# Where the residual adds of a recurrence run: two batches on GpSimd in the rounds, two on VectorE from kept states after them

## The chip, the cores and the metric

The kernel runs on one core of one Trainium2 chip. The metric is the time of one execution on the device in microseconds (us); lower is better. Before the change the median of three runs is 2685.39 us, with 2684.89 the lowest and 2687.76 the highest. The profile is that of one execution; its span, from the first to the last instruction, is 2683.1 us. Times "at 2657" are microseconds from the start of that span.

## What is computed

The input x is 4 batches of 128 channels by 64 x 64 positions, float32. Two layers follow. Layer 0 is a group norm and full self-attention over the 4096 positions, added to x. Layer 1 takes the positions as tokens: a layer norm and causal attention, added, and then a recurrence over the tokens, added as well. Cut to what the change touches:

```python
def step(yt, wx_t):
    yt = jax.nn.sigmoid(wx_t + yt @ Vt)
    return (yt, yt)
y0 = jnp.zeros((B, H), dtype=Wx.dtype)
_, ys = jax.lax.scan(step, y0, jnp.swapaxes(Wx, 0, 1))
...
t = t + _L1_attn_ref(_ln_t(t), L1_attn_Wq, L1_attn_Wk, L1_attn_Wv)
t = t + _L1_ffn_ref(_ln_t(t), L1_ffn_W, L1_ffn_V, L1_ffn_gamma, L1_ffn_beta)
```

`Wx` is the normed token times a matrix, batch-normed over all tokens. `ys` is the state after each token. What concerns us is the last sum: the state of every token is added to the token (the residual), and the sum is stored.

## The kernel before

The attention fills most of the time. It runs batch by batch in units of 256 keys for tiles of 512 queries; the scores and the weighted values go through TensorE, the exponentials through ScalarE (L441), the running sums through VectorE (L475). The reciprocals of all softmax sums are kept in `sums` (L363). The output of the attention is stored to a scratch tensor `D` in device memory (L379), and its normed product with the recurrence's input matrix takes its place in `X` (L390). Near the end of the attention `D` is loaded again into four tiles `T`, one for each batch (`residual`, L193): these are the residuals.

The recurrence stands in `chunks`. It does not walk the 4096 tokens one after the other: they are cut into `M` = 256 chunks of `L` = 16 tokens, and all 256 chunks walk together, each after a lead-in of `LEAD` = 12 tokens. A round `s`, of which there are 28 (s from -12 to 15), does one token of every chunk, for each of the four batches `b`:

- TensorE multiplies the last state by `FV` into the PSUM tile `pg` (L543),
- VectorE adds the input, `X` times `gain`, to it (L545, a fused multiply and add),
- ScalarE takes the sigmoid into the new state `Y` (L546),
- in rounds 0 to 15 the state is added to the residual in `T[b]` (L550).

The four batches are independent, so one engine works on one batch while the others work on another. Token s of chunk m lies in column 16 m + s of `T[b]`; an add of one round thus walks `T[b]` with a step of 16 elements. The states live in a pool of five buffers (`yp`), so a buffer comes free when the adds that read it are done. `lead` keeps the states of round -1.

The adds of L550 go to VectorE where `s % 4 == 3` and in the last two rounds, to GpSimd elsewhere: 20 on VectorE, 44 on GpSimd. After the last round the four tiles `T` are stored by SyncE (L553), 2 MB each. Then comes a test of the shortcut: the largest difference between the lead-in's state and the true state of the chunk before (L556 to L558), and the largest and smallest of `sums` (L564, L565). The three results are summed by TensorE (`pb`, L568) into an integer `flag` (L571). Every engine loads the flag (L580) and jumps over a slower version of the whole kernel if it is zero (L581). At the very end SyncE waits for the stores to land and a barrier closes the program.

Each engine takes its instructions in the order in which they stand in its own list. A scheduler sets that order from priorities and dependences: it had put the two maxima of `sums` (L564) far ahead of their place in the text, between the last instructions of the attention.

Of the kernel before, what the change touches and what calls it, by code (L numbers as in the profile page):

```python
# [26 lines left out]
F32 = mybir.dt.float32  # L27
AF = mybir.ActivationFunctionType
ALU = mybir.AluOpType
AX = mybir.AxisListType  # L30
PSUM = bass.MemoryType.PSUM

P = 128
# [4 lines left out]
L = 16  # L38
M = 4096 // L
LEAD = 12  # L40
# [24 lines left out]
def fast(  # L65
# [129 lines left out]
    with ExitStack() as actx:  # L195
# [317 lines left out]
        nc.vector.tensor_tensor(bias, Fbeta, bias, ALU.subtract)  # L513

    chunks(tc, X, T, gain, bias, FV, ones, sums, out, flag)


def chunks(tc, X, T, gain, bias, FV, ones, sums, out, flag):


    nc = tc.nc
    B = X.shape[1]
    with ExitStack() as ctx:
        yp = ctx.enter_context(tc.tile_pool(name="ys", bufs=5))
        keep = ctx.enter_context(tc.tile_pool(name="keep", bufs=1))
        ps_g = ctx.enter_context(tc.tile_pool(name="ps_g", bufs=1, space=PSUM))
        WX = X.rearrange("p b (c s m) -> p b c s m", s=L, c=X.shape[2] // QT)

        lead = keep.tile([P, B, M + 1], F32, name="lead")
        nc.vector.memset(lead[:, :, 0:1], 0.0)  # L530
        last = None
        for s in range(-LEAD, L):
            Y = lead[:, :, 1:] if s == -1 else yp.tile([P, B, M], F32, tag="Y", name=f"Y_{s + LEAD}")
            for b in range(B):
                wx = WX[:, b, :, s % L, :]
                y = Y[:, b, :]
                if last is None:
                    nc.scalar.activation(
                        y.rearrange("p (c m) -> p c m", c=wx.shape[1]), wx, AF.Sigmoid, bias=bias, scale=gain
                    )  # L540
                    continue
                ps = ps_g.tile([P, M], F32, tag=f"g{b}", name=f"pg_{s + LEAD}_{b}")
                nc.tensor.matmul(ps, lhsT=FV, rhs=last[:, b, :], start=True, stop=True)  # L543
                pv = ps.rearrange("p (c m) -> p c m", c=wx.shape[1])
                nc.vector.scalar_tensor_tensor(pv, wx, gain, pv, ALU.mult, ALU.add)  # L545
                nc.scalar.activation(y, ps, AF.Sigmoid, bias=bias)  # L546
                if s >= 0:
                    t = T[b].rearrange("p (m s) -> p s m", s=L)[:, s, :]
                    eng = nc.vector if s >= L - 2 or s % 4 == 3 else nc.gpsimd
                    eng.tensor_tensor(t, t, y, ALU.add)  # L550
            last = lead[:, :, :M] if s == -1 else Y
        for b in range(B):
            nc.sync.dma_start(out=out[b], in_=T[b])  # L553
        good = keep.tile([P, 4], F32, name="good")
        d = yp.tile([P, B, M - 1], F32, tag="Y", name="d")
        nc.vector.tensor_tensor(d, lead[:, :, 1:M], last[:, :, : M - 1], ALU.subtract)  # L556
        nc.vector.tensor_reduce(good[:, 0:1], d, AX.XY, ALU.max, apply_absolute_value=True)
        nc.vector.tensor_scalar(good[:, 0:1], good[:, 0:1], TOL, None, ALU.is_le)  # L558
        n = sums.shape[0]
        sums = sums.rearrange("p t j -> p (t j)")  # L560
        for i, (red, op, limit) in enumerate(
            ((ALU.max, ALU.is_le, RMAX), (ALU.min, ALU.is_ge, RMIN)), start=1
        ):
            nc.vector.tensor_reduce(good[:n, i : i + 1], sums, AX.X, red)  # L564
            nc.vector.tensor_scalar(good[:n, i : i + 1], good[:n, i : i + 1], limit, None, op)  # L565
        pb = ps_g.tile([1, 1], F32, tag="g0", name="pb")
        for i, rows in enumerate((P, n, n)):
            nc.tensor.matmul(  # L568
                pb, lhsT=good[:rows, i : i + 1], rhs=ones[:rows, 0:1], start=i == 0, stop=i == 2
            )  # L570
        nc.vector.tensor_scalar(flag, pb, -1.0, float(P + 2 * n), ALU.mult, ALU.add)  # L571
# [14 lines left out]
def whole(  # L586
# [353 lines left out]
    with ExitStack() as fctx:  # L940
# [7 lines left out]

        WX = wxp.tile([P, N, B], F32, name="WX")
        stats = wxp.tile([P, B * NQ, 6], F32, name="fstats")  # L950

        def wx_steps(b, c):
# [3 lines left out]
            nc.tensor.matmul(pw, lhsT=FW, rhs=got[0], start=True, stop=True)  # L956
            nc.scalar.copy(WX[:, ts(c, QT), b], pw)
            nc.vector.bn_stats(stats[:, b * NQ + c, :], pw)
# [21 lines left out]
        def seed(i):  # L980

            w = tmp.tile([P, TS, B], F32, tag="tmp", name=f"wn_{i}")
            nc.vector.tensor_scalar(w, WX[:, ts(i, TS), :], mv[:, 0:1], gain, ALU.subtract, ALU.mult)
            ps = ps_y.tile([P, TS, B], F32, tag="y", name=f"py_{i}")
# [8 lines left out]
        for i in range(NCH):  # L993
            Y = yp.tile([P, TS, B], F32, tag="Y", name=f"Y_{i}")
            following = None
            for s in range(TS):
                nc.tensor.matmul(
                    ps[:, s, :], lhsT=FV, rhs=last, start=False, stop=s == TS - 1, skip_group_check=True
                )
                nc.scalar.activation(Y[:, s, :], ps[:, s, :], AF.Sigmoid, bias=Fbeta)  # L1000
                last = Y[:, s, :]
                if s == TS // 2 and i + 1 < NCH:
# [44 lines left out]
```

## Time and profile before

| | before |
|---|---|
| median of 3 runs | 2685.39 us |
| span of the profile | 2683.1 us |
| TensorE busy | 2598.7 us (97%) |
| VectorE busy | 1497.6 us (56%) |
| ScalarE busy | 1118.0 us (42%) |
| GpSimd busy | 110.9 us (4%) |
| first multiply-add of round 0 (L545) | 2613.89 |
| first store issued (L553) | 2657.45 |
| flag written (L571) | 2662.89 |
| residual adds on VectorE (L550) | 20, 17.0 us |
| residual adds on GpSimd (L550) | 44, 39.3 us |

In the profile PE is TensorE, PEld its weight loads, DVE VectorE, ACT ScalarE, POOL GpSimd and SP SyncE; a `q` after the name means the engine's own queue of control instructions and DMA issues. `L550` is line 550 of the kernel. A row such as `DVE TENSOR_TENSOR T<-T,Y 128x256 f32<-128x256 f32 x3` is a group of three instructions on VectorE which write `T` and read `T` and `Y`, 128 partitions by 256 elements each; its start and the time it covers stand ahead of it. In a table by stretches each engine has its busy time and, in brackets, its number of instructions; after them come the clock that TensorE was granted, the busy share of the DMA engines, and GB/s. The chain of waits goes back from the last instruction, at each step to what released it.

### The profile page before, as it was taken

Reading aid. Unit: us, or ns where it says so; the run is one execution under the profiler, and the core shown is the slowest. Engines: PE = TensorE matmul, PEld = TensorE weight load, DVE = VectorE, ACT = ScalarE, POOL = GpSimd, SP = SyncE. Lnnn points to the kernel's source line nnn. Section 1 sums busy time; section 2 is a strip of 40 time slices with the busy share of each in tenths; the row PEclk is TensorE's granted clock in tenths of the full one; section 3 lists DMA queues with packets and bytes.
Section 4 is the critical chain, followed back from the end, with each engine's and each line's share of the span. In section 5 each row is a group of like instructions: output and inputs, shape, how many; then the busy total and the mean of one; then the engine's idle time right before and its main releaser. Section 6 shows DMA issues by size and latency. Waiting matters only on the chain.

```text
span 2683.1 us, 25668 instructions
## 1 busy us (share of the span) xinstructions
PE 2598.7 (97%) x9970; PEld 1226.6 (46%) x9970; DVE 1497.6 (56%) x2552; ACT 1118.0 (42%) x1302; POOL 110.9 (4%) x130
## 2 busy tenths in 40 slices
PE   6999999999999999999999999999999999999974
PEld 3444444445444444454444444544544444454443
DVE  4565656544555556553556565654455656555466
ACT  3444443333444444333444444334344444333353
POOL 0000000000000000000000000000000000000005
PEclk9999999999999999999999999999999999999987
DMA  3000000000000000000000000000000000100013
GB/s 133 1 1 1 1 0 12 8 5 4 5 1 1 1 1 5 12 4 9 4 1 1 1 1 1 12 8 4 5 4 1 1 0 1 67 12 8 4 67 127
DMA packets 9234, 35.81 MB, mean 13 GB/s; under 512 B 2192, under 2 KB 2960, under 8 KB 7056
## 3 DMA queue, kind: packets, MB, share of 16 engines
q1 hardware_dynamic: 6912, 33.56, 3.2%
q8 instruction: 80, 1.31, 0.2%
q10 hardware_dynamic: 2192, 0.53, 0.1%
q14 instruction: 50, 0.41, 0.0%
HBM read 17.30 MB, written 16.78 MB: 13 GB/s over the span
## 4 chain that ended last, share of the span: by engine, by line
PE 89%; DVE 7%; ACT 1%; issue 1%; DMA 0%; POOL 0%; ACTq 0%; DVEq 0%; POOLq 0%
PE av L457 47%; PE ps L428 31%; DVE tot L475 2%; DVE pg L545 1%; PE pq L319 1%; ACT s L441 1%; PE pv L313 1%; PE pk L308 1%; PE po L377 1%; PE pq L340 1%; PE pw L389 1%; DVE zt L354 1%; DVE tot L351 1%; DVE part L356 1%; PE pt L161 1%
## 5 line engine op out<-in xcount | busy, mean ns | idle before, releaser
L457 PE MATMUL av<-s,V 64*128 64x512 f32 (+3 forms) x4864 | 1361.9, 588 | 0.0
L441 ACT ACTIVATE s<-ps,shift 128x1024 f32<-128x1024 f32 (+4 forms) x796 | 808.4, 1023 | 1316.2 <-PE ps L428 1174.2
L475 DVE TENSOR_TENSOR tot<-tot,s 128x1024 f32<-128x1024 f32 (+4 forms) x796 | 878.7, 1109 | 855.5 <-ACT s L441 733.0
L428 PE MATMUL ps<-q,K 64*128 64x512 f32 (+4 forms) x3200 | 1029.3, 579 | 0.0
L457 PEld LDWEIGHTS av<-s,V 64*128 64x128 f32 (+1 forms) x4864 | 547.2, 188 | 592.3 <-issue 584.9
L428 PEld LDWEIGHTS ps<-q,K 64*128 64x128 f32 (+1 forms) x3200 | 417.0, 189 | 481.8 <-issue 470.7
L457 PE MATMUL av<-tot,V 64*128 64x512 f32 (+2 forms) x384 | 123.0, 603 | 6.1 <-DVE acc L469 5.8
L441 ACT ACTIVATE tot<-ps,shift 128x1024 f32<-128x1024 f32 (+2 forms) x68 | 71.4, 1057 | 104.3 <-PE ps L428 84.1
L155 POOL TENSOR_TENSOR rstd<-rstd,mhalf 128x4 f32<-128x4 f32 x32 | 32.2, 1007 | 1441.5 <-DVE rstd L154 1441.5
L457 PEld LDWEIGHTS av<-tot,V 64*128 64x128 f32 (+1 forms) x384 | 49.0, 188 | 70.0 <-issue 38.5
L155 POOL TENSOR_TENSOR rstd_f<-rstd_f,mhalf 128x4 f32<-128x4 f32 x32 | 33.4, 1045 | 915.3 <-DVE rstd_f L154 915.3
L543 PE MATMUL pg<-Y,FV 128*128 128x256 f32 x208 | 53.3, 418 | 16.6 <-ACT Y L546 10.0
L435 DVE TENSOR_TENSOR ps<-ps,mask 128x128 f32<-128x128 f32 x128 | 38.0, 297 | 33.8 <-PE ps L428 31.5
L174 DVE TENSOR_SCALAR V<-xt,mv,rstd 128x128 f32<-128x128 f32 x128 | 36.0, 342 | 34.4 <-POOL rstd L155 34.4
L174 DVE TENSOR_SCALAR rows<-xt_f,mv_f,rstd_f 128x128 f32<-128x128 f32 x128 | 36.7, 342 | 31.2 <-POOL rstd_f L155 31.2
L546 ACT ACTIVATE Y<-pg,bias 128x256 f32<-128x256 f32 x104 | 45.8, 474 | 18.5 <-DVE pg L545 17.9
L543 PEld LDWEIGHTS pg<-Y,FV 128*128 128x128 f32 x208 | 36.7, 205 | 34.3 <-ACT Y L546 16.9
L545 DVE SCALAR_TENSOR_TENSOR pg<-X,gain,pg 128x256 f32<-128x256 f32 x108 | 48.2, 491 | 6.9 <-PE pg L543 6.6
L354 DVE STREAM_TRANSPOSE zt<-tot 128x512 f32<-128x512 f32 x64 | 45.5, 710 | 2.1
L378 DVE TENSOR_TENSOR X<-X,po 128x512 f32<-128x512 f32 x32 | 22.0, 688 | 42.7 <-PE po L377 42.7
L351 DVE TENSOR_TENSOR tot<-tot 128x512 f32<-128x512 f32 x64 | 44.3, 692 | 2.2
L365 DVE STREAM_TRANSPOSE rt<-sums 128x512 f32<-128x512 f32 x64 | 45.0, 703 | 0.6
(127 smaller groups left out, 1133.6 us busy)
## 6 DMA issues: line engine op xcount, KB each, us to landing
X<-in_x SPq DMA_DIRECT2D x8, 1024.0 KB, 7.3
D<-X SPq DMA_DIRECT2D x32, 256.0 KB, 2.0
T<-D SPq DMA_DIRECT2D x4, 2048.0 KB, 7.8
out<-T SPq DMA_DIRECT2D x4, 2048.0 KB, 13.5
W0k<-in_w0k ACTq DMA_DIRECT2D x2, 32.0 KB, 5.1
W0q<-in_w0q ACTq DMA_DIRECT2D x2, 32.0 KB, 4.8
W0v<-in_w0v ACTq DMA_DIRECT2D x1, 64.0 KB, 5.3
W1q<-in_w1q ACTq DMA_DIRECT2D x1, 64.0 KB, 7.3
```

The source lines that it names most:

```text
L155: nc.gpsimd.tensor_tensor(dst, dst, mhalf[:, :n], ALU.pow)
L174: nc.vector.tensor_scalar(rows[:, j, :], xt[:, j, :], mv[:, j, 0:1], rstd[:, j : j + 1], ALU.subtract, ALU.mult)
L351: nc.vector.tensor_tensor(both, both, total[:, 1, :], ALU.add)
L354: nc.vector.transpose(zt.rearrange("p j a -> p (j a)"), both)
L365: nc.vector.transpose(rt.rearrange("p (j a) -> p j a", a=R), r.unsqueeze(2).to_broadcast([P, QT // R, R]))
L428: nc.tensor.matmul(ps[:, h, first[h] :], lhsT=K[layer, b][rows, ts(2 * u + h, P)], rhs=Q[t][rows, first[h] :], start=True, stop=True,)
L441: nc.scalar.activation(s[:, *a], ps[:, *a], AF.Exp, bias=shift[layer, b])
L457: nc.tensor.matmul(acc[:, first[h] :], lhsT=V[layer, b][rows, 2 * u + h, :], rhs=s[rows, h, first[h] :], start=u == 0 and h == 0, stop=u = ...
L475: nc.vector.tensor_tensor(total[:, *a], total[:, *a], s[:, *a], ALU.add)
L543: nc.tensor.matmul(ps, lhsT=FV, rhs=last[:, b, :], start=True, stop=True)
L545: nc.vector.scalar_tensor_tensor(pv, wx, gain, pv, ALU.mult, ALU.add)
L546: nc.scalar.activation(y, ps, AF.Sigmoid, bias=bias)
```

## The change

The adds are divided by batch and no longer by round. Batches 0 and 1 are added by GpSimd in every round. The states of batches 2 and 3 are written by ScalarE into a tile of their own, `later`, that keeps all 16 rounds; after the last round VectorE adds them in eight instructions of 128 x 1024 (16 rounds by 64 chunks), while the first two batches are stored. The stores of batches 2 and 3 are cut in halves, each issued when two of the eight adds are done. The differences of the test are taken batch by batch, since the last states now lie in two tiles. The words `tc.keep_in_program_order` hold an instruction at its place in the text on its engine, so that the test, with the two maxima of `sums`, comes after the eight adds. The purpose is to keep the adds out of VectorE's rounds and to start the stores of two batches without waiting for the other two.

```diff
+        half = B // 2
+        later = keep.tile([P, B - half, L, M], F32, name="later")
...
         for s in range(-LEAD, L):
-            Y = lead[:, :, 1:] if s == -1 else yp.tile([P, B, M], F32, tag="Y", name=f"Y_{s + LEAD}")
+            if s == -1:
+                Y = [lead[:, b, 1:] for b in range(B)]
+            else:
+                y = yp.tile([P, half if s >= 0 else B, M], F32, tag="Y", name=f"Y_{s + LEAD}")
+                Y = [
+                    later[:, b - half, s, :] if s >= 0 and b >= half else y[:, b, :] for b in range(B)
+                ]
...
-                nc.scalar.activation(y, ps, AF.Sigmoid, bias=bias)
-                if s >= 0:
+                nc.scalar.activation(Y[b], ps, AF.Sigmoid, bias=bias)
+                if s >= 0 and b < half:
                     t = T[b].rearrange("p (m s) -> p s m", s=L)[:, s, :]
-                    eng = nc.vector if s >= L - 2 or s % 4 == 3 else nc.gpsimd
-                    eng.tensor_tensor(t, t, y, ALU.add)
-            last = lead[:, :, :M] if s == -1 else Y
+                    nc.gpsimd.tensor_tensor(t, t, Y[b], ALU.add)
+            last = [lead[:, b, :M] for b in range(B)] if s == -1 else Y
+        for b in range(half):
+            nc.sync.dma_start(out=out[b], in_=T[b])
+        for b in range(half, B):
+            t = T[b].rearrange("p (m s) -> p s m", s=L)
+            for i in range(4):
+                cols = ts(i, M // 4)
+                tc.keep_in_program_order(
+                    nc.vector.tensor_tensor(
+                        t[:, :, cols], t[:, :, cols], later[:, b - half, :, cols], ALU.add
+                    )
+                )
+                if i % 2:
+                    cols = ts(i // 2, M * L // 2)
+                    nc.sync.dma_start(out=out[b][:, cols], in_=T[b][:, cols])
+        good = keep.tile([P, 4], F32, name="good")
+        d = keep.tile([P, B, M - 1], F32, name="d")
         for b in range(B):
-            nc.sync.dma_start(out=out[b], in_=T[b])
-        good = keep.tile([P, 4], F32, name="good")
-        d = yp.tile([P, B, M - 1], F32, tag="Y", name="d")
-        nc.vector.tensor_tensor(d, lead[:, :, 1:M], last[:, :, : M - 1], ALU.subtract)
+            tc.keep_in_program_order(
+                nc.vector.tensor_tensor(d[:, b, :], lead[:, b, 1:M], last[b][:, : M - 1], ALU.subtract)
+            )
...
-            nc.vector.tensor_reduce(good[:n, i : i + 1], sums, AX.X, red)
+            tc.keep_in_program_order(nc.vector.tensor_reduce(good[:n, i : i + 1], sums, AX.X, red))
```

More of the change, by code (lines that the diff above doesn't have):

```diff
@@ L532, in chunks @@
         for s in range(-LEAD, L):
-            Y = lead[:, :, 1:] if s == -1 else yp.tile([P, B, M], F32, tag="Y", name=f"Y_{s + LEAD}")
+            if s == -1:
[5 more added lines that the diff above has]
+                ]
             for b in range(B):
                 wx = WX[:, b, :, s % L, :]
-                y = Y[:, b, :]
                 if last is None:
                     nc.scalar.activation(
-                        y.rearrange("p (c m) -> p c m", c=wx.shape[1]), wx, AF.Sigmoid, bias=bias, scale=gain
+                        Y[b].rearrange("p (c m) -> p c m", c=wx.shape[1]), wx, AF.Sigmoid, bias=bias, scale=gain
                     )
@@ L542, in chunks @@
                 ps = ps_g.tile([P, M], F32, tag=f"g{b}", name=f"pg_{s + LEAD}_{b}")
-                nc.tensor.matmul(ps, lhsT=FV, rhs=last[:, b, :], start=True, stop=True)
+                nc.tensor.matmul(ps, lhsT=FV, rhs=last[b], start=True, stop=True)
                 pv = ps.rearrange("p (c m) -> p c m", c=wx.shape[1])
                 nc.vector.scalar_tensor_tensor(pv, wx, gain, pv, ALU.mult, ALU.add)
-                nc.scalar.activation(y, ps, AF.Sigmoid, bias=bias)
-                if s >= 0:
+                nc.scalar.activation(Y[b], ps, AF.Sigmoid, bias=bias)
+                if s >= 0 and b < half:
                     t = T[b].rearrange("p (m s) -> p s m", s=L)[:, s, :]
-                    eng = nc.vector if s >= L - 2 or s % 4 == 3 else nc.gpsimd
-                    eng.tensor_tensor(t, t, y, ALU.add)
-            last = lead[:, :, :M] if s == -1 else Y
+                    nc.gpsimd.tensor_tensor(t, t, Y[b], ALU.add)
[16 more added lines that the diff above has]
+        d = keep.tile([P, B, M - 1], F32, name="d")
         for b in range(B):
-            nc.sync.dma_start(out=out[b], in_=T[b])
-        good = keep.tile([P, 4], F32, name="good")
-        d = yp.tile([P, B, M - 1], F32, tag="Y", name="d")
-        nc.vector.tensor_tensor(d, lead[:, :, 1:M], last[:, :, : M - 1], ALU.subtract)
+            tc.keep_in_program_order(
+                nc.vector.tensor_tensor(d[:, b, :], lead[:, b, 1:M], last[b][:, : M - 1], ALU.subtract)
+            )
         nc.vector.tensor_reduce(good[:, 0:1], d, AX.XY, ALU.max, apply_absolute_value=True)
```

## The prediction

> **What bounds the kernel now.** I read the 40 slices first, then the tail by stretches, then the order of time on VectorE and GpSimd, the chain of waits, and last the queue of the store engine and the branch at the end. The slices show TensorE at 9 tenths until slice 38: the attention fills all but the last 4%, and the diff does not touch it. So only the last 115 us matter. This is the recurrence by stretches (columns: length, busy time and instructions of each engine, granted clock, DMA share, GB/s):
>
> ```profile
> 2600.00:2612.00 12.00, 12.00 (x55) 8.01 (x54) 12.00 (x28) 11.95 (x28) 0.00 (x0) 1.00 0.00 0
> 2612.00:2620.00 8.00, 8.00 (x37) 5.42 (x37) 7.98 (x19) 7.91 (x19) 5.03 (x7) 1.00 0.00 0
> 2620.00:2657.00 37.00, 26.64 (x99) 18.35 (x98) 34.52 (x66) 21.46 (x50) 34.24 (x38) 0.90 0.00 1
> ...
> 2660.00:2664.00 4.00, 0.29 (x6) 0.21 (x6) 2.50 (x4) 0.00 (x0) 0.00 (x0) 0.50 1.08 455
> 2664.00:2668.00 4.00, 0.00 (x0) 0.00 (x0) 0.00 (x0) 0.00 (x0) 0.00 (x0) 0.50 0.95 397
> ```
>
> The reader is to see three stages. Up to 2620 VectorE runs one fused multiply-add after the other and everything else fits beside it; then the residual adds join it and the rate of rounds falls; after 2657 nothing runs but four stores. VectorE in that order of time (start, length):
>
> ```profile
> 2611.60 9.01 DVE L545 SCALAR_TENSOR_TENSOR pg<-X,gain,pg 128x256 f32<-128x256 f32 x20
> 2620.52 2.84 DVE L550 TENSOR_TENSOR T<-T,Y 128x256 f32<-128x256 f32 x3
> 2623.20 1.26 DVE L545 SCALAR_TENSOR_TENSOR pg<-X,gain,pg 128x256 f32<-128x256 f32 x3
> ...
> 2657.67 0.96 DVE L545 SCALAR_TENSOR_TENSOR pg<-X,gain,pg 128x256 f32<-128x256 f32 x2
> 2658.78 1.08 DVE L550 TENSOR_TENSOR T<-T,Y 128x256 f32<-128x256 f32 x2
> 2659.77 1.21 DVE L556 TENSOR_TENSOR d<-lead,Y 128x1020 f32<-128x1020 f32 x1
> ```
>
> Three adds hold VectorE for 2.84 us while GpSimd also adds; two take 1.08 us at 2658.78, when GpSimd is done. GpSimd itself does seven in 5.73 us before the first of them:
>
> ```profile
> 2614.97 5.73 POOL L550 TENSOR_TENSOR T<-T,Y 128x256 f32<-128x256 f32 x7 [25.87 <-ACT Y L546]
> ```
>
> At the end the store queue waits (engine, waited for: total, times, longest) and every engine jumps over the fallback. The waits of SyncE:
>
> ```profile
> SPq L581 <- SPq L581: 16.7, 1, 16.7
> ```
>
> The same line by instruction (durations in ns, then first and last start):
>
> ```profile
> L581 PEldq COMPARE_BRANCH  x1: 7430/7430/7430, 2664.3 to 2664.3; - x1
> L581 SPq COMPARE_BRANCH  x1: 50/50/50, 2664.5 to 2664.5; - x1
> ...
> L581 DVEq EVENT_SEMAPHORE  x1: 21/21/21, 2671.9 to 2671.9; - x1
> ```
>
> SyncE is past its branch at 2664.5 and waits 16.7 us for the stores, to 2681.2. The other engines are back from their jump at 2671.9, 9.3 us before that. Today the stores set the end; the flag has 9.3 us to spare.
>
> [...] 0.95 us an add in the group of three, 0.54 alone, while the multiply-adds (one input in PSUM) keep 0.45 us apart beside GpSimd. [...] T is walked with a step of 16 elements, 64 bytes, and the add of 256 that stands alone takes 0.585 us where a contiguous one (L475, 128x256) takes 0.426. [...] no run yet shows the jump with the DMA idle.
>
> **The change, part by part.**
>
> 1. *The two maxima over the reciprocal sums leave the middle.* In the chain `rt` ends at 2571.93, then "DVE good L564" and 0.96 us of issue stand before `u` at 2572.95. In the new order they come after the last test. `u` starts at about 2571.96: 1.0 us off the path, and all that follows moves by as much. The second maximum lies beside the matmul of `po` and frees nothing; the moved memset of `lead` lies beside TensorE. All times below include this 1.0.
>
> 2. *Twenty residual adds leave VectorE in the rounds, twelve net leave GpSimd.* VectorE then has 64 multiply-adds only. Rate: 53 in 23.81 us, 0.449 each, a round of four 1.79. The first of round 0 starts at 2613.9 in the chain, so at 2612.9; 64 x 0.448 = 28.7 gives 2641.6. Before, the last ended at 2658.6, so this is 16.0 us less besides the 1.0. GpSimd has two adds a round at 0.82 us (5.73 / 7), 1.64 of 1.79: it keeps up, and five Y buffers cover lateness. The states of batches 2 and 3 go to `later`, never reused, so no wait is added.
>
> 3. *The first two stores.* The last state of batch 0 is ready at about 2640.8, GpSimd adds it by 2641.7, and the store of batch 0 is issued then, against 2657.45. Before, issue of the first store to the wake of SyncE took 2681.2 - 2657.45 = 23.75 us for 8.4 MB, continuous. The same gives 2665.4, if the DMA never runs dry.
>
> 4. *Eight adds of 128x1024 on VectorE.* No row has this shape. Low bound 1.23 us, a contiguous 1024 (L475); high bound 4 x 0.59 = 2.37, four of the small adds. Contiguous adds of 128, 256 and 512 elements take 0.285, 0.426 and 0.693, hence 0.15 fixed plus 1.06 ns an element; the strided one gives (0.585 - 0.15) / 256 = 1.70 ns. I take 0.15 + 1.74 = 1.9 us. Eight are 15.2: 2641.6 to 2656.8. [...] The quarters of 1 MB are handed out near 2645.4, 2649.2, 2653.0 and 2656.8, while the first two stores alone hold the DMA to about 2652.5 (4.2 MB near 0.4 MB/us after 0.8 us of start), so it does not run dry: at 2.37 the last comes at 2660.6, still in time for 2665.4.
>
> 5. *The flag comes later.* Queued behind the eighth add on VectorE: four differences of 255 (1.5, up to 0.42 each), their maximum and test (1.25 + 0.2), the two moved maxima and tests (2 x 1.35), matmul and flag (0.62 as before from the test's end), load of the flag up to the branch (2663.04 to 2664.34, 1.3). Sum 7.6: branch at 2664.4. Then the jump: 7.5 us as now is the high end, 2.0 us (what a 256 KB store from D took to land) the low one. The stores have little left by then, so I take 3.2: the engines are back at 2667.6. Event, drain and the last barrier took 0.2 + 0.7: end 2668.5. The store path needs 2665.4 + 1.9 (2681.2 to 2683.1, the waits behind it) = 2667.3. So the flag, not the stores, ends last, by about 1 us.
>
> Sum: 16.0 + 1.0 gained, 2.4 given back in the tail (2683.1 - 2668.5 = 14.6). The median stands 2.3 over the profiled span (2685.39 - 2683.1): 2670.8 us.
>
> **The rivals.**
>
> A: the stores end last, 2667.3 + 2.3 = 2669.6. For it: the DMA is never idle, and adds of 1.7 us would pull the flag forward by 1.6. Against: a jump made during the stores waits behind their packets, as now.
>
> B: the jump costs its full 7.5. End 2664.4 + 7.5 + 0.9 = 2672.8, time 2675.1. For it: the only jump seen took that. Against: the stores would be nearly done.
>
> C: GpSimd becomes the bound. [...] 32 adds from 2614.0 take 35.8, to 2649.8, and the first stores move by about 7.4 us: 2669.6 + 7.4 = 2677.0. Against: no VectorE instruction with two SBUF inputs is left in the rounds.
>
> D, slower: the long strided adds are far worse than 256 of them suggest. The flag path ends at 2653.3 + 8 x A; it passes 2683.1 at A = 3.7. At four times the slowest contended group (three adds in 3.28 us at 2630.87, 1.09 each), 4.4 us, it is 2688.5, time 2690.8. For it: the pattern is not in the trace. Against: same steps in both operands, and GpSimd is silent by then.
>
> **How the numbers follow.** Forecast 0.57, A 0.18, B 0.15, C 0.05, D 0.05. The range takes in A with a store tail 1.6 us better (2668.0) and B (2675.1), and ends at 2675.5; outside remain C, D and the far ends. Faster means under about 2680: all but D, and of D some part is below the old time, so 0.95 faster, 0.01 same, 0.04 slower.
>
> **What would show it.** Right: multiply-adds 0.45 us apart through round 15; the first store issued near 2641.7; eight adds near 1.9 us; DMA share near 1 to about 2664; the branch near 2664 and the other engines back after SyncE's wait for the stores has ended. Wrong: GpSimd starts over 1.7 us a round apart, adds over 2.4 us, gaps in the DMA between the third and sixth store, or `u` still waiting 1 us behind a maximum.

## The result and the profile after

The changed kernel takes 2673.34 us (2672.82 to 2673.89, 4 runs) against 2685.47 us for the kernel before (2684.89 to 2687.76, 4 runs) on the same chip: ratio 0.9953, 95% interval 0.9936 to 0.9971, 12.1 us less. The forecast was 2670.8, with a range of 2668.0 to 2675.5. The direction and the mechanism hold; 2.5 us of the gain are missing. The profiled span is 2671.3 us where 2668.5 was forecast, so the profile holds the whole of the miss (2.8), and it can be looked for there.

The tail by stretches, to be laid beside the one of before (columns: length, busy time and instructions of PE, PEld, DVE, ACT and POOL, granted clock, DMA share, GB/s):

```profile
2612.00:2623.00 11.00, 11.00 (x50) 7.53 (x50) 10.94 (x25) 10.87 (x25) 7.83 (x10) 1.00 0.00 0
2623.00:2642.00 19.00, 19.00 (x84) 14.02 (x83) 18.34 (x43) 17.52 (x42) 17.21 (x21) 1.00 0.00 1
2642.00:2658.00 16.00, 0.32 (x2) 0.00 (x0) 15.89 (x11) 1.36 (x4) 3.33 (x3) 0.65 0.89 377
2658.00:2664.00 6.00, 0.57 (x6) 0.29 (x6) 5.37 (x11) 0.00 (x0) 0.00 (x0) 0.50 0.95 393
2664.00:2668.00 4.00, 0.00 (x0) 0.00 (x0) 0.00 (x0) 0.00 (x0) 0.00 (x0) 0.50 0.06 12
2668.00:2671.00 3.00, 0.00 (x0) 0.00 (x0) 0.00 (x0) 0.00 (x0) 0.00 (x0) 0.50 0.05 14
```

Three things are to be seen. The rounds end at 2643 and not at 2659. From 2642 to 2664 VectorE and the DMA work side by side, which is what the change is for. And the last 7 us are empty on every engine, with the DMA at 0.05: here nobody computes and nothing is stored, and still the kernel isn't done. Before, stores moved to within 3 us of the end, with a thin last part:

```profile
2676.00:2680.00 4.00, 0.00 (x0) 0.00 (x0) 0.00 (x0) 0.00 (x0) 0.00 (x0) 0.50 0.60 246
```

The order of time on VectorE, GpSimd and the store queue (start, length, engine, line, what, count):

```profile
2611.78 30.64 DVE L554 SCALAR_TENSOR_TENSOR pg<-X,gain,pg 128x256 f32<-128x256 f32 x67
...
2623.71 1.67 POOL L558 TENSOR_TENSOR T<-T,Y 128x256 f32<-128x256 f32 x2 [0.17 <-ACT Y L555]
...
2642.20 3.32 POOL L558 TENSOR_TENSOR T<-T,Y 128x256 f32<-128x256 f32 x2 [0.19 <-ACT Y L555]
...
2642.96 15.04 DVE L567 TENSOR_TENSOR T<-T,later 128x1024 f32<-128x1024 f32 x8
2643.08 2.81 SPq L561 DMA_DIRECT2D out<-T  x2
2647.32 11.04 SPq L573 DMA_DIRECT2D out<-T  x4
2657.93 0.72 DVE L578 TENSOR_TENSOR d<-lead,Y 128x255 f32<-128x255 f32 x2
...
2660.65 1.21 DVE L587 TENSOR_REDUCE good<-sums 128x1 f32<-128x1024 f32 x1
...
2663.64 0.15 DVE L594 TENSOR_SCALAR flag<-pb 1x1 int32<-1x1 f32 x1 [0.28 <-PE pb L591]
```

VectorE does its multiply-adds without a break. GpSimd starts its pairs 1.85 us apart and not 1.79: a small slip to which experiment e6 comes. The eight adds take 1.88 us each on the mean (15.04 / 8), forecast 1.9. The pair of GpSimd at 2642.20 took 3.32 us where others take 1.67: its second add ran from 2643.00 to 2645.52, beside and beyond the first long add of VectorE (2642.96 to 2644.85). That cost GpSimd 1.65, and VectorE's next long add took 2.55 us where the median is 1.87. Of the stores the second alone was delayed, while the first one already fills the DMA (share 1.16 from 2643.9, its first data, to 2645.5).

At the end, the waits of SyncE (waited for: total, times, longest):

```profile
SPq L1066 <- DVEq L604: 2.6, 1, 2.6
```

Line 604 is the branch over the fallback (line 581 before). Before, SyncE waited 16.7 us for the stores. Now no wait for the stores is left in that list; SyncE waits for the engines that jump. The branch by instruction (durations in ns, then first and last start):

```profile
L604 SPq EVENT_SEMAPHORE  x8: 17/17/17, 2664.8 to 2665.4; - x8
...
L604 PEldq COMPARE_BRANCH  x1: 3633/3633/3633, 2664.4 to 2664.4; - x1
...
L604 ACTq EVENT_SEMAPHORE  x1: 17/17/17, 2667.7 to 2667.7; - x1
...
L604 POOLq EVENT_SEMAPHORE  x1: 17/17/17, 2668.8 to 2668.8; - x1
```

The eight events of SyncE, its waits for transfers, pass from 2664.8 to 2665.4 without a stop: the stores are in. The last engine is back from its jump at 2668.8, four microseconds later. So the flag's chain ends last, as forecast. The jump costs 3.3 us on ScalarE and 4.1 on GpSimd, where it cost 7.4 before. Then comes a part that the forecast had not seen. The closing barrier, line 1066:

```profile
L1066 SPq EVENT_SEMAPHORE  x10: 17/28/2542, 2665.4 to 2669.6; - x10
...
L1066 PEldq EVENT_SEMAPHORE  x2: 51/51/51, 2669.1 to 2671.2; - x2
```

SyncE is through at 2669.6; TensorE's second event stands at 2671.2, and with it the span ends. In the kernel before, the same two ended together, at 2683.1:

```profile
L1043 SPq EVENT_SEMAPHORE  x10: 17/28/28, 2681.8 to 2683.1; - x10
...
L1043 PEldq EVENT_SEMAPHORE  x2: 51/51/51, 2682.6 to 2683.1; - x2
```

The DMA view has packets of a kind of their own after the branch, "instruction", taken here for the instructions that the jump fetches. Kernel before, from the branch to 2669.0 (queue, kind: packets, MB, share of 16 engines):

```profile
q1 hardware_dynamic: 140, 2.03, 103.6%
```

and from 2669.0 to 2672:

```profile
q1 hardware_dynamic: 73, 1.20, 100.5%
q8 instruction: 1, 0.02, 2.1%
q14 instruction: 3, 0.02, 1.9%
```

Changed kernel, from the branch at 2664.4 to 2668, and from 2668 to 2671.2:

```profile
q14 instruction: 4, 0.03, 4.7%
q8 instruction: 1, 0.02, 2.0%
```

```profile
q14 instruction: 3, 0.02, 2.9%
q8 instruction: 1, 0.02, 2.1%
```

Before, the fetched instructions move only 4.7 us after the branch (2664.34 to 2669.05), and 2 MB of stores pass in between; with the DMA empty they move after 0.9 us (first packet at 2665.36, branch at 2664.43). And there are two groups of them: one after the branch (2665.4 to 2667.4 in the changed kernel), one when the engines are back. Before, the second group ran at 2675.3 to 2677.1, beside the stores, and no engine waited for it. Now it runs from 2668.3 to 2669.9, in the open.

### The profile page after: what moved, and what is told of

It is laid out like the page before. It is cut to its first block, busy times and chain, and to the rows that moved or that the text cites. A ratio compares the mean times of both kernels' runs of the same rounds, so it can differ in the third digit from the quotient of the medians.

```text
span 2671.3 us, 25646 instructions
## 1 busy us (share of the span) xinstructions
PE 2595.3 (97%) x9970; PEld 1222.3 (46%) x9970; DVE 1498.2 (56%) x2543; ACT 1118.8 (42%) x1302; POOL 100.1 (4%) x118
## 4 chain that ended last, share of the span: by engine, by line
PE 91%; DVE 6%; ACT 1%; issue 1%; DMA 0%; POOL 0%; ACTq 0%; DVEq 0%; POOLq 0%
PE av L457 47%; PE ps L428 32%; PE pg L552 2%; DVE tot L475 2%; PE pq L319 1%; ACT s L441 1%; PE pv L313 1%; PE pk L308 1%; PE po L377 1%; PE pq L340 1%; PE pw L389 1%; DVE zt L354 1%; DVE tot L351 1%; DVE part L356 1%; PE pt L161 1%
## 5 line engine op out<-in xcount | busy, mean ns | idle before, releaser
L441 ACT ACTIVATE s<-ps,shift 128x1024 f32<-128x1024 f32 (+4 forms) x796 | 809.2, 1024 | 1315.3 <-PE ps L428 1172.0
L356 DVE TENSOR_REDUCE part<-zt 128x16 f32<-128x512 f32 x64 | 43.9, 686 | 2.1
L552 PE MATMUL pg<-Y,FV 128*128 128x256 f32 x148 | 38.7, 410 | 6.5 <-ACT Y L547 6.5
L363 DVE RECIPROCAL sums<-pz 128x16 f32<-128x16 f32 x64 | 16.4, 256 | 46.7 <-PE pz L361 46.7
```

Of the source, the lines that this page charges most:

```text
L356: nc.vector.tensor_reduce(part, zt, AX.X, ALU.add)
L441: nc.scalar.activation(s[:, *a], ps[:, *a], AF.Exp, bias=shift[layer, b])
L552: nc.tensor.matmul(ps, lhsT=FV, rhs=last[b], start=True, stop=True)
```

## The experiments

All times are medians beside runs of the kernel before on the same chip, whose medians were 2684.9 to 2685.5.

| run | what | us | ratio to before, 95% |
|---|---|---|---|
| e1 | before, maxima moved to the end | 2684.35 | 0.9998 [0.9989, 1.0007] |
| e2 | no late adds | 2661.94 | 0.9915 [0.9899, 0.9932] |
| e3 | maxima three times | 2678.50 | 0.9976 [0.9967, 0.9984] |
| e4 | before, no adds on GpSimd | 2678.61 | 0.9976 [0.9966, 0.9986] |
| e5 | no late adds, stores in order | 2672.36 | 0.9950 [0.9935, 0.9966] |
| e6 | 13 state buffers | 2672.40 | 0.9955 [0.9942, 0.9969] |
| e7 | maxima ahead of the rounds | 2672.37 | 0.9961 [0.9947, 0.9975] |
| e8 | e7, test ahead of the adds | 2671.93 | 0.9950 [0.9936, 0.9964] |
| e9 | the changed kernel again | 2674.21 | 0.9959 [0.9946, 0.9973] |
| e10 | e6 and e7 together | 2672.07 | 0.9948 [0.9934, 0.9961] |
| e11 | e8 with 13 buffers | 2670.66 | 0.9948 [0.9935, 0.9962] |
| e12 | e11, test between the adds | 2670.33 | 0.9945 [0.9931, 0.9958] |

### e1: the order of the maxima alone

```diff
-            nc.vector.tensor_reduce(good[:n, i : i + 1], sums, AX.X, red)
+            tc.keep_in_program_order(nc.vector.tensor_reduce(good[:n, i : i + 1], sums, AX.X, red))
```

> The kernel before with one edit: the two maxima of the reciprocal sums stay at their place in the text, after the test of the states, and no longer stand in the middle. My theory: u starts 0.9 us earlier and everything after it with it; the flag comes 2.6 us later but has 9.3 us to spare, since the stores set the end. So 0.9 us faster than before, about 2684.5. Rival one: the maxima in the middle cost nothing: no change. Rival two: the flag's lateness counts: 1.7 us slower.

Measured 0.5 us less, and the interval takes in no change: the time alone doesn't resolve it. The chain of waits does, at this place. Before:

```profile
2571.22 0.71 DVE rt L365
2571.93 0.06 DVE good L564
2571.99 0.96 issue
2572.95 0.69 DVE u L367
```

In this run `u` follows `rt` at once:

```profile
2571.59 0.72 DVE rt L365
...
2572.41 0.70 DVE u L367
```

0.10 us stand between them, against 1.02 before (0.06 and 0.96). So the step of 1.0 is right in place and near in size (0.92). It didn't reach the end in full: the data of the stores begin only 0.2 us earlier than before (2658.05 against 2658.28). Part of the reason is in the section on the prediction, step 1. The flag came 2.2 us later here and cost nothing, since SyncE still waited 14.1 us for the stores.

### e4: the adds of both engines at once

```diff
-                    eng = nc.vector if s >= L - 2 or s % 4 == 3 else nc.gpsimd
-                    eng.tensor_tensor(t, t, y, ALU.add)
+                    if s >= L - 2 or s % 4 == 3:
+                        nc.vector.tensor_tensor(t, t, y, ALU.add)
```

> The kernel before with the 44 adds of GpSimd left out, so most of the states are not added; VectorE keeps its 20. My theory, that VectorE's adds are slow in the rounds [...]: they fall from 0.93 us to about 0.58, a group of three from 2.84 us to about 1.6, and the end comes 4 to 9 us earlier than before. Rival, that an add of 64-byte steps is as slow by itself: no change.

6.3 us less. The first group of VectorE's adds, with GpSimd silent:

```profile
2622.95 1.62 DVE L550 TENSOR_TENSOR T<-T,Y 128x256 f32<-128x256 f32 x3
```

Three adds take 1.62 us where they took 2.84 before. What GpSimd's adds cost is measured here: 0.4 us on each add of VectorE (0.95 us beside them, 0.54 with GpSimd silent). With 20 adds on VectorE that is up to 8 us; the whole kernel gained 6.3. In the traces rounds 0 to 15 took 44.7 us before, 36.9 here and 29.2 in the changed kernel.

Not all of the first difference comes from the two engines adding at once. In the rounds of before, TensorE's granted clock fell to 0.5 twice, for 3.4 us each; in those of the changed kernel it stayed at 1.0, and in those of e4 too, up to their last microsecond. Two rounds of before in which VectorE adds nothing, the first of them at half clock (columns as above):

```profile
2636.62:2639.87 3.25, 3.10 (x8) 2.40 (x8) 1.87 (x5) 2.23 (x6) 3.25 (x5) 0.53 0.00 0
2639.87:2641.72 1.85, 1.85 (x9) 1.42 (x8) 1.78 (x4) 1.41 (x5) 1.85 (x3) 1.00 0.00 0
```

That round alone lost 1.4 us. So of some 16 us that the change takes out of the rounds, about 6 come of VectorE and GpSimd no longer adding at once, 1.4 or somewhat more stood at half clock, and the rest, 7.6, are the 20 adds themselves. Whether the clock would have fallen without the slower adds, no run tells.

### e2 and e5: without the eight late adds

Both leave the adds of batches 2 and 3 out. In e5 their stores are also held behind the first two:

```diff
-                tc.keep_in_program_order(
-                    nc.vector.tensor_tensor(
-                        t[:, :, cols], t[:, :, cols], later[:, b - half, :, cols], ALU.add
-                    )
-                )
...
-                    nc.sync.dma_start(out=out[b][:, cols], in_=T[b][:, cols])
+                    tc.keep_in_program_order(nc.sync.dma_start(out=out[b][:, cols], in_=T[b][:, cols]))
```

> The changed kernel with the eight adds of batches 2 and 3 left out, so those two batches are stored without their states. My theory, that the eight adds, the flag and the jump set the end of the changed kernel: the flag comes 15 us earlier, the stores set the end again, and with first issue to landing as before (21 to 24 us) the span ends at 2666 to 2669, 2 to 5 us under the changed kernel. The jump is then made while the stores run and takes about 7 us again, against 3.4 to 4.1 in the changed kernel. Rival, the stores set the end of the changed kernel: no change, 2673. Rival on the jump, that its length has nothing to do with the stores: 3.4 to 4.1 here too.

> The changed kernel with the eight adds of batches 2 and 3 left out, so those two batches are stored without their states, and with their four stores held behind the first two (in the run before they went out ahead of the recurrence). My theory: the stores alone now set the end: first issue near 2643.3 and 20.5 to 23.8 us to the landing, then 1.9, so a span of 2666 to 2669, 2 to 5 us under the changed kernel; the jump, made while the stores run, takes over 6 us and is hidden. Rival (the stores set the end of the changed kernel): no change.

e2 tells less than it was made for. Without the adds nothing held the four stores of batches 2 and 3; they went out at 2576 to 2588, ahead of the recurrence, and only two were left for the end. Its 2661.94 us is a kernel with half of the stores gone from the tail, not one with cheaper adds. e5 mends this, and its expectation of a clear gain failed: 2672.36, 1.0 below the changed kernel. The stores of this run by stretches:

```profile
2650.00:2658.00 8.00, 0.19 (x2) 0.09 (x2) 0.97 (x3) 0.00 (x0) 0.00 (x0) 0.50 1.03 419
2658.00:2664.00 6.00, 0.00 (x0) 0.00 (x0) 0.00 (x0) 0.00 (x0) 0.00 (x0) 0.50 0.99 404
2664.00:2670.00 6.00, 0.00 (x0) 0.00 (x0) 0.00 (x0) 0.00 (x0) 0.00 (x0) 0.50 0.36 145
```

VectorE is idle but for the test, all six stores are queued by 2650.1, and yet their data runs from 2645.7 to 2669.3, with a thin end (0.36). In the changed kernel it runs from 2643.9 to 2663.9. The packets' own time, summed over the 16 DMA engines and divided by 16, is 20.4 and 20.0 us. So the changed kernel's stores run without a gap, and those of e5 take 3.5 us more, at the end, where not all of the 16 have work. (The trace of e5 was also 1.8 us later by its first store, 2644.87 against 2643.08.) What follows: the eight adds cost the stores nothing, and taking them away wins next to nothing, since the stores then last longer.

Two things could make them last longer. In e5 they are queued within 5.3 us; in the changed kernel the last four are handed out 3.5 us apart. And in e5 the jump comes early (branch at 2652.6), so that the instructions that it fetches move among the stores, in two groups from 2656.8 and from 2662.4 on; in the changed kernel they move after them. The traces of all runs speak for the second. Where the fetches came after the stores (after, e3, e6, e7, e9, e10), the data of the 8.4 MB took 20.0 to 20.1 us. Where they fell among them (before, e1, e4, e5, e8, e11, e12), it took 22.2 to 23.5, in e8, e11 and e12 too, which hand out their last four stores one by one (with one hole between two of them). And the last two stores of e2, issued within 1.3 us, end without a thin part; there the first fetched instructions moved at 2654.5:

```profile
2652.00:2654.00 2.00, 0.00 (x0) 0.00 (x0) 0.00 (x0) 0.00 (x0) 0.00 (x0) 0.50 0.98 393
2654.00:2656.00 2.00, 0.00 (x0) 0.00 (x0) 0.00 (x0) 0.00 (x0) 0.00 (x0) 0.50 0.12 25
```

No run changes the one and holds the other, so that the fetches lengthen the stores is likely and not shown.

### e3: a longer flag chain

```diff
-            tc.keep_in_program_order(nc.vector.tensor_reduce(good[:n, i : i + 1], sums, AX.X, red))
+            for _ in range(3):
+                tc.keep_in_program_order(nc.vector.tensor_reduce(good[:n, i : i + 1], sums, AX.X, red))
```

> The changed kernel with each of the two maxima of the sums taken three times, so four more reductions of 1.2 us stand ahead of the flag, long after the last store is issued. My theory (the flag sets the end): 4.9 to 5.1 us slower than the changed kernel, about 2678.3, and the jump, now made with the DMA idle from its start, still takes 3.3 us or a little more. Rival (the stores set the end): under 1 us of change.

5.2 us more than the changed kernel (2678.50 against 2673.34; 4.3 more than its second measurement, e9) for four more maxima of 1.21 us and what lies between them: what is added to the chain of the flag appears in full in the time. The traces agree: the first store is 2.2 us later here, the branch 7.2 and the end of the span 7.4. That the flag and not the stores sets the end is shown by this. It also gives the price of the jump long after the stores, which had ended at 2666.2:

```profile
L605 PEldq COMPARE_BRANCH  x1: 3473/3473/3473, 2671.6 to 2671.6; - x1
```

3.5 us here, 3.6 in the changed kernel (3.8 and 4.0 in e9 and e6, whose stores had ended too), 7.4 before. Five microseconds of silence on the DMA made it hardly cheaper; in the four traces whose stores had ended the jump took 3.5 to 4.0 us on TensorE.

### e6: the slip in the rounds

ScalarE writes a state buffer again that two engines have read: GpSimd for its add, and VectorE's chain through the matmul. In this run batches 0 and 1 have 13 buffers, so that reuse begins only in round 13.

```diff
-        yp = ctx.enter_context(tc.tile_pool(name="ys", bufs=5))
+        yp = ctx.enter_context(tc.tile_pool(name="ys", bufs=13))
...
-                y = yp.tile([P, half if s >= 0 else B, M], F32, tag="Y", name=f"Y_{s + LEAD}")
-                Y = [
-                    later[:, b - half, s, :] if s >= 0 and b >= half else y[:, b, :] for b in range(B)
-                ]
+                if s >= 0:
+                    y = yp.tile([P, half, M], F32, tag="Y", name=f"Y_{s + LEAD}")
+                    Y = [later[:, b - half, s, :] if b >= half else y[:, b, :] for b in range(B)]
+                else:
+                    k = (s + LEAD) % (L // 2)
+                    Y = [later[:, b // half, 2 * k + b % half, :] for b in range(B)]
```

> The changed kernel with 13 instead of 5 buffers for the states of batches 0 and 1 (the states of the lead-in use the room of the kept states). In the changed kernel each round from 5 on is 1.85 us and not 1.79, and ScalarE has one more waiting instruction in it, for GpSimd to have left the buffer. My theory: that extra instruction lies on the loop through the four engines; with 13 buffers only rounds 13 to 15 have it, 8 rounds fewer by 0.062: the last state comes 0.5 us earlier, the time falls by about 0.5. Rival: VectorE or TensorE is simply slower beside GpSimd's adds: rounds stay at 1.85.

The sigmoid's line by instruction, in the changed kernel:

```profile
L555 ACTq EVENT_SEMAPHORE  x11: 17/17/17, 2623.1 to 2641.6; - x11
```

and with 13 buffers:

```profile
L557 ACTq EVENT_SEMAPHORE  x3: 17/17/17, 2636.9 to 2640.6; - x3
```

ScalarE gets one more instruction per round, an event of its own for the second engine that it must wait for, from round 5 on, and three with 13 buffers, from round 13 on. The kernel before has such events too (nine, from 2626.4), in the rounds that the adds slowed anyway. The wait has long been met: each event takes 17 ns. Even so the round goes from 1.79 to 1.85 us: rounds 5 to 13 took 14.79 us in the changed kernel (2623.16 to 2637.95) and 14.37 here (2622.55 to 2636.92). And in this run the rounds go to 1.84 and 1.85 us where the events come back, in rounds 13 and 14. The one round of 1.85 us ahead of them in the changed kernel, the last of the run-up, has an event as well, in TensorE's queue at 2612.8; with 13 buffers this event is missing and the round takes 1.79. 0.06 us in each of 11 rounds is 0.65 us. The time of the whole, 0.9 below that of the changed kernel in another set of runs, is at the edge of what can be told; the trace carries this reading.

### e7, e8, e10, e11, e12: where the test stands

In e7 the two maxima with their tests stand ahead of the rounds, where VectorE waits anyway (3.29 us ahead of its first multiply-add in the changed kernel). In e8 the whole test and the flag come ahead of the eight adds as well. e10 and e11 are e7 and e8 with the 13 buffers of e6. In e12 the test stands between the adds of batch 2 and those of batch 3. The core of it, as e12 has it:

```diff
         keep = ctx.enter_context(tc.tile_pool(name="keep", bufs=1))
...
+        good = keep.tile([P, 4], F32, name="good")
...
+        for i, (red, op, limit) in enumerate(
+            ((ALU.max, ALU.is_le, RMAX), (ALU.min, ALU.is_ge, RMIN)), start=1
+        ):
+            tc.keep_in_program_order(nc.vector.tensor_reduce(good[:n, i : i + 1], sums, AX.X, red))
...
-        for b in range(half, B):
+        def late(b):
...
+        late(half)
...
         nc.vector.tensor_scalar(flag, pb, -1.0, float(P + 2 * n), ALU.mult, ALU.add)
+        for b in range(half + 1, B):
+            late(b)
```

> The changed kernel with the two maxima of the sums between the last scalar of the batch norm and the first round, where VectorE waits 3.3 us for ScalarE and TensorE. They need 2.7 us there, so the rounds start as before, and the flag comes 2.6 us earlier. Theory one, a jump of fixed length: 2.6 us faster. Theory two, mine, that the jump waits for the stores' packets: the branch now falls before the stores have ended, the jump takes 5 to 7 us, and 0.5 to 1.5 us are gained. Rival (stores set the end): no change.

e7: the flag comes 2.3 us earlier (2661.37), but the time falls by 1.0 (four runs from 2671.69 to 2672.66; the fifth took 2681.95, and no trace shows why). The jump stands under the end of the stores again, whose last event at SyncE is at 2665.2:

```profile
L604 PEldq COMPARE_BRANCH  x1: 4033/4033/4033, 2662.8 to 2662.8; - x1
```

and the load of the flag takes 1.2 us where it took 0.54 in the changed kernel. Of 2.3 us, 0.66 go to the load and about 0.4 to 0.6 to the jump.

> As the run before, and the test of the states and the flag come before the eight adds. TensorE, ScalarE and GpSimd then jump while VectorE still adds; only VectorE jumps after the adds[...]. If the end is set by VectorE's chain, VectorE leaves its adds at about 2661.2, as late as the flag in the run before, and jumps 4 to 6 us; but TensorE's late last wait (1.5 us after the others in the changed kernel) should be gone. I expect 2 to 3.5 us under the changed kernel, about 2670 to 2671. If the stores set the end, it is slower: the last store is issued 3 us later.

e8: 2671.93, 1.4 below the changed kernel, less than expected. Branch at 2648.0, jump 6.9 to 8.6 us, all of it under the adds and the stores. Now the stores end last: the last one is issued at 2661.12, the data ends at 2667.1, the span at 2669.3. The early test had its price on the DMA: the third store came 6.6 us after the second, and the fetches fell among the stores, whose data took 23.4 us.

> The changed kernel itself, beside the three variants below, so that they are compared with it in the same hour and not only through the kernel before. Theory: 2673.3 us, within 0.7. Rival (times drift between calls by as much as the small differences read here): more than 1 us away from 2673.3, in which case gains under 1 us in the other runs mean nothing.

e9: 2674.21 (2673.67 to 2675.51), 0.9 above the first measurement of the same kernel. It lies between the two lines of its expectation: sets of runs differ by nearly 1 us. So the single gains of e6 and e7, 0.9 and 1.0 across sets, aren't told from this drift by the time alone.

> The changed kernel with both small edits: 13 state buffers, and the two maxima with their tests between bias and rounds. Theory (the flag's chain sets the end and both savings lie on it): 0.5 us less in the rounds and about 1.0 us at the end, together 1.5 less than the changed kernel, 2671.8, with the branch near 2662.4. Rival (stores end last once the flag comes earlier): the first store goes out 0.5 us earlier, and the time falls by no more than that, 2672.8.

e10: 2672.07, between the two times of its expectation; but it is 2.1 below e9, the changed kernel in the same set, more than the 1.5 of its theory. SyncE's last event for a transfer is at 2666.5 and it ends at 2669.7, so the flag is still last.

> The whole test ahead of the eight long adds, with the maxima ahead of the rounds and 13 state buffers. Theory: the stores end last here (last one handed out 2661.1 in the run with 5 buffers, data to 2667.1), and the last add with them moves up by the 0.5 us of the rounds: 2671.4. Rival (the stores take the same time whatever starts them): no gain on the run with 5 buffers, 2671.9.

e11: 2670.66 (2669.76 to 2672.82), 3.6 below e9 and below both times of its expectation.

> As the run before, but the test stands between the four long adds of batch 2 and the four of batch 3. Theory: the stores of batch 2 then go out at about 2645.5 and 2649 and keep the DMA full until 2658; the test takes VectorE from 2648.5 to 2653.8; the branch comes near 2655 and its jump of 7 to 8 us under the stores ends near 2663, hidden; batch 3's quarters go out near 2657.5 and 2661, data to about 2665, end of the span 2667.5, time about 2669.5 to 2670.5. Rival (a jump under stores grows as long as the stores last, 8.6 us and more): the engines come back near 2665, barrier after them, 2671.5 to 2672. A time of 2673 or more would refute both.

e12: 2670.33 (2670.03 to 2670.77, 5 runs), 3.9 below e9 (no run of one in the range of the other) and 14.9 below the kernel before in this set (2685.18). Its theory's time holds, its rival's does not. It is the fastest complete version that was run; e11 isn't told from it. In order of time:

```profile
2641.95 7.94 DVE L577 TENSOR_TENSOR T<-T,later 128x1024 f32<-128x1024 f32 x4
2646.37 14.34 SPq L583 DMA_DIRECT2D out<-T  x4
...
2653.10 0.15 DVE L598 TENSOR_SCALAR flag<-pb 1x1 int32<-1x1 f32 x1 [0.47 <-PE pb L595]
2653.18 7.17 DVE L577 TENSOR_TENSOR T<-T,later 128x1024 f32<-128x1024 f32 x4
```

and its branch:

```profile
L610 PEldq COMPARE_BRANCH  x1: 6350/6350/6350, 2654.5 to 2654.5; - x1
...
L610 POOLq EVENT_SEMAPHORE  x1: 17/17/17, 2661.8 to 2661.8; - x1
```

The flag is out at 2653.1 and the jump ends at 2661.8, while VectorE adds batch 3 until 2660.4. The stores end the span: data to 2666.1, SyncE's last transfer event at 2666.9, end at 2668.3. What it still loses is in the DMA, whose share falls to 0.84 from 2658 to 2662 and 0.51 from 2662 to 2666; the first fetched instructions moved at 2658.1, and the stores' data took 23.2 us.

### The end of the program

The time of a profiled execution is a little longer than the last event of SyncE in its trace. By how much depends on where the jump lay:

| run | SyncE's last event | time of that execution | between | the jump |
|---|---|---|---|---|
| before | 2683.1 | 2684.9 | 1.8 | under stores |
| e5 | 2671.4 | 2673.2 | 1.8 | under stores |
| e8 | 2669.2 | 2671.0 | 1.8 | under stores |
| e12 | 2668.2 | 2670.0 | 1.8 | under stores |
| after | 2669.6 | 2672.8 | 3.2 | last |
| e3 | 2677.0 | 2680.3 | 3.3 | last |
| e7 | 2668.5 | 2671.7 | 3.2 | last |
| e6 | 2668.5 | 2672.3 | 3.7 | last |
| e10 | 2669.7 | 2672.6 | 2.9 | last |

The other five traces agree: 1.8 to 1.9 in e1, e4 and e11 (under stores), 3.1 in e2 and about 3.7 in e9 (last). A jump that ends last costs 1.1 to 1.9 us again after the barrier. In e6 and e10 TensorE's event isn't late in the trace and the time is nevertheless. That the second group of fetched instructions is the cause fits the DMA view, before and after, but no run takes that group away; it stays argued.

## Why the prediction was right, and where 2.5 us went

The sum came within 2.5 us of the result with errors of both signs. By its steps, each against the profiled span:

| point of the forecast | forecast | measured | added to the miss |
|---|---|---|---|
| first multiply-add of round 0 | 2612.9 | 2613.63 | +0.7 |
| last multiply-add ends | 2641.6 | 2642.85 | +0.5 |
| first long add starts | 2641.6 | 2642.96 | +0.1 |
| eight adds done | 2656.8 | 2657.93 | -0.2 |
| branch | 2664.4 | 2664.4 | -1.1 |
| last engine back | 2667.6 | 2668.8 | +1.2 |
| end of the span | 2668.5 | 2671.3 | +1.6 |

*Step 1, the maxima leave the middle.* Right at its place: 0.92 us in the trace (e1: 0.92 too). The chain of the changed kernel:

```profile
2571.47 0.72 DVE rt L365
...
2572.28 0.70 DVE u L367
```

0.7 us of it are lost again before round 0: `rt` ends 0.26 later in this trace (2572.19 against 2571.93), and the run-up rounds took 21.33 us where they took 20.93 (2592.30 to 2613.63; 2592.96 to 2613.89 before). The first is within what single traces differ by (`rt` starts between 2571.1 and 2573.7 in the traces of all runs). The second is a term that the forecast did not have: TensorE's granted clock. It was 0.5 when the run-up began and rose to 1.0 at 2595.5, against 2595.3 before; the earlier start of the rounds did not bring it earlier. So 3.2 us of the run-up lay at half clock and not 2.4. In all 14 traces the length of the run-up follows this time: 20.90 us with 2.3 at half clock (e4), 21.33 with 3.2, 21.54 with 3.7 (e1), 21.75 with 4.1 (e9).

*Step 2, the rounds.* Right in rate and in mechanism, with GpSimd keeping up as worked out (1.67 us a pair). The words that failed are "so no wait is added". Buffers did cover lateness: nobody is late. But a buffer that a second engine reads brings an event instruction on ScalarE, and that instruction alone cost 0.06 us a round (1.85 us with it, 1.79 without) in a loop in which four engines hand one value round (e6). The rate of 1.79 was read from the run-up, where no buffer is read by GpSimd, and so the forecast counted waiting and not the instruction that waits: 0.65 us, of which 0.5 show in the table (the 28.7 us had a little slack). All that the rounds of before lost was put down to the adds; the part of it that stood at half clock (e4) was overlooked, at no cost to the forecast.

*Step 3, the stores.* The first store was forecast for 2641.7 and went out at 2643.08. They landed at 2664.8, 21.7 us later and not 23.75. The stores from which the 23.75 was read were not "continuous" to the end: their data took 22.5 us (2658.3 to 2680.8) with a thin last part, where those of the changed kernel took 20.0. The jump's fetches, which lay among the stores before and come after them now, are the likely reason (e5). So rival A was further off than its 0.18 said: the stores were done 4.0 us before the last engine was back.

*Step 4, the adds.* 1.88 against 1.9 a piece. Splitting the cost into a fixed part and one per element, with the strided figure taken from the trace of before, gave an unseen shape within 2%. The strided figure of 1.70 ns an element held for four times the length: (1.88 - 0.15) / 1024 = 1.69.

*Step 5, the flag.* Three terms were mis-sized, and two of them compensated. The sum of 7.6 us up to the branch measured 6.5: 0.65 of the difference is the load of the flag (0.54 us with the stores ending, 1.19 under them), 0.2 is the matmul with the flag, two of whose three parts were done beforehand, and 0.2 the differences with their maximum and test. The jump of 3.2 was taken near its low end (which is the time of a 256 KB store into D, not from it); it measured 3.3 to 4.1 by engine, and the barrier waits for the slowest, GpSimd: 4.4 from the branch to its return. The largest miss is the term "Event, drain and the last barrier took 0.2 + 0.7": it measured 2.5. It was read from a program whose jump lay under the stores. There the second group of fetches lay under them too, and with the stores gone it comes into the open (see the table above). The DMA view of the changed kernel shows both after the one branch at 2664.4: 5 packets from 2665.4 on, and 4 from 2668.3 on.

*The rivals.* B, the full jump of 7.5, is refuted: 3.6 us on TensorE, and e3 confirms it. Its time, 2675.1, is nevertheless closer to the result (1.8 us) than the forecast's (2.5), by a cost that B didn't contain. C is refuted by 1.67 us a pair. D is refuted by 1.88 us an add. The last step, from span to median, was 2.3 in the forecast and 2.0 in the result. (The execution whose profile was read took 2684.87, so 0.5 of the 2.3 was a difference between executions.)

## What to carry to other kernels

When a transfer stops setting the end, everything that it had hidden comes due at its own price: here a jump, two groups of instruction fetches and a barrier, about 7.5 us between the flag and the end. Price those terms for the new place and not from the trace in which they were hidden, and then ask whether the work that leads to them can stand earlier; moving the test between two groups of adds brought 3.9 us (e12, with two smaller edits). Hiding the jump may have a price too: wherever its fetches fell among the stores, the stores took 2 to 3.5 us longer (22.2 to 23.5 against 20.0 to 20.1), though it was not shown that the fetches are the cause. Before giving a buffer a second reader in a tight loop, count the instruction that waits for it, even where the wait is always met (0.06 us a round here).

## What the runs showed of the hardware

- A jump over about 460 lines of program took 3.3 to 4.2 us with the DMA idle (after, e3), 4.0 to 4.6 with the stores about to end (e7), and 6.1 to 8.6 while stores filled it (before, e8, e12). After the branch the DMA view shows packets of the kind "instruction": 9 in the changed kernel, 0.09 MB.
- The load of one word of the flag took 0.54 us with the stores about at their end (after) and 1.2 under them (before, e7).
- A wait for a second engine cost one more instruction in ScalarE's queue and 0.06 us a round, though it was always met (after, e6).
- Beside the first long add of VectorE with two SBUF inputs (1.89 us) a GpSimd add took 2.52 us where the median is 0.86; the next long add took 2.55 (median 1.87; after).
- Three adds of VectorE, with two SBUF inputs each, took 2.84 us (0.95 each) beside GpSimd's adds and 1.62 us (0.54 each) with GpSimd silent (before, e4).
- Stores of the same 8.4 MB moved in 20.0 to 20.1 us in the six traces in which the jump's fetches came after them, and in 22.2 to 23.5 us in the seven in which they fell among them. The packets' time per DMA engine was 20.0 to 20.1 and 20.2 to 20.4 us; the end was uneven. How the stores were handed out does not sort the traces so; the cause was not isolated.
- A round at a granted clock of 0.5 took 3.25 us, and the next one, at 1.0, 1.85 us (before). The half clock at the start of the rounds ended 2.3 to 4.1 us after the first multiply-add, and the run-up took 20.90 to 21.75 us in the same order (14 traces).
